# Attention and mixture of experts on one core: theta built from a row, scatters ahead of the turn's late work, unused expert rows masked on VectorE, y's zeros written later, the last layer norms through a square root

## The chip, the core and the metric

The kernel runs on one core of a Trainium2 chip. The time is device microseconds from start to end of one execution on that core; of several runs the median is given. The profile is of one further execution, taken by the hardware profiler.

## What is computed

Sixteen sequences of 512 tokens, 128 channels, all float32. The reference, cut to what matters:

```python
q = silu(x @ Wq); k = silu(x @ Wk); v = x @ Wv           # 16 heads of 8
q, k = lrpe(q), lrpe(k)                # concat(t * cos(pos * theta), t * sin(pos * theta))
out = ((q @ k.T) * tril) @ v           # no softmax
out = layernorm((out @ Wo) * sigmoid(x @ G1 @ G2)) * gamma + beta
x1 = layernorm(x + out)
logits = (x1 * rsqrt(mean(x1 * x1) + eps)) @ router_w.T   # 8 experts
topk_p, topk_i = top_k(softmax(logits), 2); rw = topk_p / sum(topk_p)
# each expert takes, in token order, its first capacity = 1280 tokens
routed[token] += rw * (silu(xg @ rg) * (xg @ ru)) @ rd    # xg: the expert's rows
shared = (silu(x1 @ sg) * (x1 @ su)) @ sd
result = layernorm(x1 + shared + routed)
```

## The kernel before

**Stages.** The work is cut in chunks of 128 tokens, four to a sequence, NT = 64 in all. A prologue (L199 to L344) makes constants. The main loop (L737 to L778) runs the attention with t from -2 to 64 as a software pipeline: turn t projects chunk t+2 (L359: two matmuls into pq, six ScalarE operations, and on VectorE hat, the queries and keys times cosine and sine), turns over chunk t+1 (L393: transposes pt, five ScalarE copies), makes the energies of chunk t (L435: sixteen matmuls pe, four VectorE maskings et by `causal`), the values of chunk t-1 (L457: pout) and the state of chunk t+1 (L412: pst, masked on VectorE, added to the last state on POOL at L433). When a sequence's four chunks are through, a generator `after(b)` (L495) is stepped on once or twice a turn: output projection, gate, two layer norms, the mean square, the transposes px1 into x1T, the router's logits. The reciprocal roots there (r, r2, rms) are powers on POOL (L109, L542). `route` (L566) is a generator too, stepped by `sprinkle`, one small VectorE operation after another: softmax, the two best experts, a running count per expert, and the slot of each token's row in its two experts.

**Rows to the experts.** `scatter` (L669) sends one chunk's rows, 132 words each (128 channels, the token's number, the tag of its first expert, two weights), to their slots in `xg_dram` by an indirect DMA that POOL issues; 128 of these are needed. `scatter_behind` issues one, and may put a small multiplication (`beat`) ahead of it on POOL, which holds it until a given column is ready. In the loop the two scatters of a turn stand last, behind `advance` and `sprinkle`.

**The shared expert as filling.** `feed` is a list of short TensorE steps (gate pg, up pu, down pd; L113 to L157). `shared(t)` in the loop takes one where it is due, twice a turn. What is left over runs after the routed experts.

**Fills.** Every expert has 1280 slots, and fewer tokens may come. Before the scatters, `fill` (L350) writes `xg_dram` with `empty`, rows of zeros with 1.0e6 as their token's number (8 DMAs of 660 KB), and `y_dram` with `zero` (8 DMAs of 1 MB), both from SP's queue, one in each of the turns 0 to 15. An unused slot's row thus comes to the expert as zeros, and its result is dropped at L862 since its target lies beyond the rows of y.

**The experts** (L924 to L951). `load_expert` (L813) loads the weights and the 1280 rows `xg` of an expert. `turn_rows` (L826) transposes 512, 512 or 256 of them on TensorE (ept) and copies the result to xgT on VectorE. Each expert works in three parts of these sizes (L933); a part has four steps i, each with a gate matmul peg, an up matmul peu, a Silu on ScalarE and the product eh on VectorE (L945), and then one entry of `backs` (the down projection ped of an earlier part with its scatter home, L850) and one of `aside`. In the middle part of expert e, `aside` holds the three `turn_rows` of expert e+1 and its `targets_of` (L836: the token's target row and weight).

**The end** (L953 to L983). The rest of `feed` runs, `add_up` adds the routed rows, and `finish_lot` (L897) makes the last layer norm: statistics, reciprocal root by `rstd_of` (L105: an addition on VectorE and a power on POOL), nb, and `res` on ScalarE. Lots are of four chunks, the last sequence's of one.

**What sets the order.** `manual_schedule(engines=ORDERED)` (L199, L736, L924) makes TensorE, ScalarE, VectorE and POOL execute in the order of the program's text; ORDERED (L18) has no SP, whose DMA issues the scheduler places. Waits between engines and for buffers come from the tiles.

**The prologue's lines.** theta is loaded to all partitions at once (L201). W comes by ScalarE's queue (L204), and eight columns of each head in it are filled with the product of the gate's two factors (pg12, L308; copy at L335). POOL clears `rw_sb`, the four padded value tiles (L287 to L295), `goes_on`, `zero` and `empty`, and builds the masks. The angle table (L315 to L337) is made for chunk 0 and then for chunks 1 to 3 together, and the sines and cosines on ScalarE; copies at L338 fill in the columns that are the same.

Of the kernel before, what the change touches and what calls it, by code (L numbers as in the profile page):

```python
# [28 lines left out]
NOBODY = 1.0e6  # L29
# [6 lines left out]
C1 = 6.28125  # L36
C2 = 2029.0 / 2 ** 20
C3 = 2.0 * math.pi - C1 - C2
# [9 lines left out]
def tile_kernel(  # L48
# [37 lines left out]
    nc.gpsimd.memset(neghalf, -0.5)  # L86
    x1 = keep.tile([P, NT, R], F32, name="x1")
# [5 lines left out]
    idx = keep.tile([P, 2, NT], I32, name="idx")  # L93
    sg_sb = keep.tile([P, IS], F32, name="sg_sb")
# [10 lines left out]
    def rstd_of(var, n, eps):  # L105
        ve = small.tile([P, n], F32, tag="ve", name="ve")
        nc.vector.tensor_scalar(ve, var, eps, None, ALU.add)  # L107
        r = small.tile([P, n], F32, tag="rstd", name="rstd")
        nc.gpsimd.tensor_tensor(r, ve, neghalf[:, :n], ALU.pow)  # L109
        return r  # L110


    def shared_steps(b):  # L113
# [6 lines left out]
        def gate_half(i):  # L120
# [7 lines left out]
            h["s", i] = sl  # L128

# [30 lines left out]
    done = set()  # L160
    latest = [None]
# [15 lines left out]
    with ExitStack() as ph:  # L177
# [21 lines left out]
        with tc.manual_schedule(engines=ORDERED):  # L199
            th_sb = cst.tile([P, D + HALF], F32, name="th_sb")  # L200
            nc.sync.dma_start(th_sb, theta.partition_broadcast(P))  # L201
# [3 lines left out]
            load_xT(0)  # L205
            g1t_sb = cst.tile([8, D], F32, name="g1t_sb")
            nc.scalar.dma_start(g1t_sb, g1t)
            g2_sb = cst.tile([8, D], F32, name="g2_sb")
            nc.scalar.dma_start(g2_sb, g2)
# [7 lines left out]
            nc.gpsimd.memset(rw_sb, 0.0)  # L217
# [3 lines left out]
            load_x(1)  # L221
# [3 lines left out]
            nc.sync.dma_start(bet, beta.partition_broadcast(P))  # L225

# [19 lines left out]
            expi = cst.tile([P, E], I32, name="expi")  # L246
            nc.gpsimd.iota(expi, pattern=[[1, E]], base=0, channel_multiplier=0)
            expf = cst.tile([P, E], F32, name="expf")
            nc.vector.tensor_copy(expf, expi)
            first = cst.tile([P, E], F32, name="first")  # L250
            nc.vector.tensor_scalar(first, expf, -1.0, float(E), ALU.mult, ALU.add)
            startrow = cst.tile([P, E], F32, name="startrow")
            nc.vector.tensor_scalar(startrow, expf, float(CAP), float(-NSLOT), ALU.mult, ALU.add)
            count = cst.tile([P, E], F32, name="count")
            nc.vector.memset(count, 0.0)
            goes_on = {}
            for n in sorted({(b1 - b0) * NC for b0, b1 in groups}):
                goes_on[n] = cst.tile([P, E, n + 1], F32, name=f"goes_on{n}")
                nc.gpsimd.memset(goes_on[n], 1.0)
                nc.gpsimd.memset(goes_on[n][:, :, 0], 0.0)  # L260


            ones = cst.tile([P, P], F32, name="ones")
            nc.vector.memset(ones, 1.0)

            causal = cst.tile([P, 3, HALF], F32, name="causal")
            nc.gpsimd.memset(causal, 1.0)
            for block, at in ((0, 0), (0, HALF), (1, HALF), (2, 0)):
                rows = causal[at : at + HALF, block, :]
                nc.gpsimd.affine_select(  # L270
                    rows, rows, pattern=[[1, HALF]], compare_op=ALU.is_ge, fill=0.0, base=0, channel_multiplier=-1
                )
            tri = cst.tile([P, P], F32, name="tri")
            nc.gpsimd.affine_select(
                tri, ones, pattern=[[1, P]], compare_op=ALU.is_gt, fill=0.0, base=0, channel_multiplier=-1
            )
# [7 lines left out]
            )  # L284


            NVP = 4  # L287
            vpads = []
            for i in range(NVP):
                vp = cst.tile([P, 4, 4, 40], F32, name=f"vpad{i}")  # L290
                nc.gpsimd.memset(vp, 0.0)

                vl = cst.tile([P, 8, 40], F32, name=f"vlow{i}")
                nc.gpsimd.memset(vl, 0.0)
                vpads.append((vp, vl))  # L295


            toki = cst.tile([P, NT], I32, name="toki")
            nc.gpsimd.iota(toki, pattern=[[P, NT]], base=0, channel_multiplier=1)
            zero = hp.tile([P, 4 * N], F32, tag="h", name="zero")  # L300
            nc.gpsimd.memset(zero, 0.0)
            empty = hp.tile([P, NS, R], F32, tag="h", name="empty")
            nc.gpsimd.memset(empty, 0.0)
            nc.gpsimd.memset(empty[:, :, D], NOBODY)


            pg = ps_w.tile([P, D], F32, tag="w", name="pg12")
            nc.tensor.matmul(pg, g1t_sb, g2_sb, start=True, stop=True)  # L308

            cst_tok = cst.tile([P, NC, 2, 16, 2, 8], F32, name="cst_tok")
            scratch = hp.tile([P, 2, NC, D + HALF], F32, tag="h", name="scratch")
            ang, turns_ = scratch[:, 0], scratch[:, 1]
            for c0, c1 in ((0, 1), (1, NC)):  # L315
# [6 lines left out]
                for part in (C1, C2, C3):  # L322
                    nc.vector.scalar_tensor_tensor(a, k, -part, a, ALU.mult, ALU.add)
# [26 lines left out]
        def fill(i):  # L350
            if i < 8:
                nc.sync.dma_start(y_rows[:, i, :], zero)
            elif i < 16:
                nc.sync.dma_start(x_rows[:, i - 8, :], empty.rearrange("p r d -> p (r d)"))
# [674 lines left out]
```

## Time and profile before

| what | us |
|---|---|
| median of 3 runs (888.18 to 888.76) | 888.75 |
| the profiled execution | 912.27 |
| its span | 910.6 |
| busy in the span: TensorE matmul (PE) | 843.0 (93%) |
| TensorE weight load (PEld, beside matmuls) | 576.5 (63%) |
| VectorE (DVE) | 557.1 (61%) |
| ScalarE (ACT) | 442.3 (49%) |
| GpSimd (POOL) | 344.2 (38%) |

The mean granted TensorE clock of that execution was 0.981. DMA moved 62.97 MB. In the trace the first energies (pe) start at 25.4, the experts' first peg at 534.3, and the last addition of routed rows on VectorE (to x1T) ends at 888.8.

The page's rows of digits cut the span into 40 equal slices; a digit is the busy share in tenths. A line of a stretch gives from and to, its length, the busy time and count of instructions of PE, PEld, DVE, ACT and POOL, the granted clock, the DMA engines' busy share and GB/s. A line of the timeline gives start, duration, engine, line and operation, out<-in, shapes, and in brackets how long the engine had been idle and what it waited for. TensorE's weight loads (LDWEIGHTS) stand apart from their matmuls; PE and SP are TensorE and SyncE.

### The profile page before, as it was taken

The page shows a single profiled execution, that of the slowest core. Times are in us where ns is not written, and L with a number is a line of the kernel's source. Part 1 is how long each engine was busy: PE and PEld are TensorE (multiplying, and loading weights), DVE is VectorE, ACT ScalarE, POOL GpSimd, SP SyncE. Part 2 cuts the span into 40 slices and gives each one's busy share as a digit, 9 for nine tenths or more (in the row PEclk, how much of TensorE's full clock was granted, in tenths as well). Part 3 has the DMA queues.
Part 4 walks back from the last instruction along what each step waited for, and adds up shares of the span by engine and source line. Part 5 has one row for each costly group of instructions (what it writes and reads, how often), then busy time and mean ns, then how long its engine had stood idle before and what let it go on. Part 6 is the DMA issues. An engine that isn't in the chain of part 4 may idle for free.

```text
span 910.6 us, 24496 instructions
## 1 busy us (share of the span) xinstructions
PE 843.0 (93%) x9790; PEld 576.5 (63%) x9790; DVE 557.1 (61%) x1687; ACT 442.3 (49%) x1285; POOL 344.2 (38%) x455
## 2 busy tenths in 40 slices
PE   2898999999998999989999999999999999999990
PEld 1676667666755776674566657776677766666670
DVE  6588788987688788878743333333333325884542
ACT  3677677566576757745522223333333332334332
POOL 4023222155655645566666703333333331010011
PEclk9999999999999999999999999999999999999996
DMA  8941111011111111000000053222231004641001
GB/s 288 417 146 33 31 32 32 24 34 55 44 50 50 55 32 39 26 22 22 12 8 2 2 159 94 77 68 60 84 91 62 27 24 125 177 135 34 25 24 46
DMA packets 64338, 62.97 MB, mean 69 GB/s; under 512 B 6179, under 2 KB 55130, under 8 KB 63200
## 3 DMA queue, kind: packets, MB, share of 16 engines
q1 hardware_dynamic: 57392, 50.44, 17.5%
q0 software_dynamic: 6656, 10.69, 3.7%
q8 instruction: 77, 1.26, 0.6%
q14 instruction: 37, 0.30, 0.1%
q10 hardware_dynamic: 176, 0.27, 0.1%
HBM read 32.71 MB, written 31.88 MB: 71 GB/s over the span
## 4 chain that ended last, share of the span: by engine, by line
PE 78%; DVE 14%; issue 3%; ACT 3%; DMA 1%; POOL 0%; POOLq 0%; DVEq 0%; ACTq 0%
PE pd L143 11%; PE pg L125 11%; PE pu L133 11%; PE ped L856 8%; PE peg L940 8%; PE peu L942 8%; PE pe L444 4%; PE pq L363 4%; DVE et L451 4%; PE pout L486 3%; PE pt L399 2%; PE pout L477 2%; PE pout L468 1%; PE po L501 1%; DVE st L101 1%
## 5 line engine op out<-in xcount | busy, mean ns | idle before, releaser
L109 POOL TENSOR_TENSOR rstd<-ve,neghalf 128x4 f32<-128x4 f32 (+1 forms) x51 | 52.4, 1028 | 259.0 <-DVE ve L107 224.0
L671 POOL DMA_INDIRECT xg_dram<-x,idx x128 | 132.2, 1033 | 37.7 <-issue 32.1
L127 ACT ACTIVATE sl<-pg 128x512 f32<-128x512 f32 x128 | 76.0, 596 | 127.6 <-PE pg L125 113.2
L862 POOL DMA_INDIRECT y_dram<-y,to x80 | 77.6, 970 | 154.2 <-ACT y L860 154.2
L945 DVE TENSOR_TENSOR eh<-esl,peu 128x512 f32<-128x512 f32 (+1 forms) x96 | 57.5, 599 | 128.1 <-PE peu L942 123.7
L125 PE MATMUL pg<-x1T,sg_sb 128*128 128x512 f32 x256 | 134.0, 605 | 2.1 <-DVE h L134 0.9
L451 DVE TENSOR_TENSOR et<-pe,causal 128x384 f32<-128x384 f32 x256 | 124.4, 547 | 18.0 <-PE pe L444 17.8
L134 DVE TENSOR_TENSOR h<-sl,pu 128x512 f32<-128x512 f32 x128 | 87.6, 684 | 75.5 <-PE pu L133 57.6
L133 PE MATMUL pu<-x1T,su_sb 128*128 128x512 f32 x256 | 131.4, 595 | 0.4 <-DVE x1T L148 0.4
L143 PEld LDWEIGHTS pd<-sd_sb,h 128*128 128x128 f32 x1024 | 119.6, 193 | 5.5 <-issue 5.5
L143 PE MATMUL pd<-sd_sb,h 128*128 128x128 f32 x1024 | 122.6, 276 | 0.0
L856 PEld LDWEIGHTS ped<-rd,eh 128*128 128x128 f32 x640 | 84.0, 192 | 24.6 <-issue 22.7
L940 PE MATMUL peg<-xgT,rg 128*128 128x512 f32 (+1 forms) x192 | 84.6, 522 | 0.0
L942 PE MATMUL peu<-xgT,ru 128*128 128x512 f32 (+1 forms) x192 | 84.4, 521 | 0.0
L856 PE MATMUL ped<-rd,eh 128*128 128x128 f32 x640 | 84.3, 275 | 0.0
L944 ACT ACTIVATE esl<-peg 128x512 f32<-128x512 f32 (+1 forms) x96 | 50.5, 526 | 56.0 <-PE peg L940 53.9
L133 PEld LDWEIGHTS pu<-x1T,su_sb 128*128 128x128 f32 x256 | 46.1, 192 | 45.8 <-issue 39.3
L860 ACT ACTIVATE y<-ped,wt 128x128 f32<-128x128 f32 x80 | 29.4, 367 | 84.6 <-PE ped L856 79.9
L125 PEld LDWEIGHTS pg<-x1T,sg_sb 128*128 128x128 f32 x256 | 44.8, 193 | 39.0 <-issue 33.9
L363 PE MATMUL pq<-W,xT 128*128 128x384 f32 x128 | 61.5, 564 | 7.8 <-DVE W L335 6.9
L444 PE MATMUL pe<-q,kT 32*64 32x192 f32 x2048 | 61.9, 338 | 0.8 <-issue 0.8
L386 DVE TENSOR_TENSOR hat<-qk,cst_tok 128x512 f32<-128x512 f32 x64 | 45.5, 711 | 23.3 <-ACT qk L371 22.6
(164 smaller groups left out, 1285.6 us busy)
## 6 DMA issues: line engine op xcount, KB each, us to landing
y_dram<-zero SPq DMA_DIRECT2D x8, 1024.0 KB
y<-y_dram SPq DMA_DIRECT2D x32, 256.0 KB, 3.2
xT<-xt SPq DMA_DIRECT2D x16, 384.0 KB, 6.5
xg_dram<-empty SPq DMA_DIRECT2D x8, 660.0 KB, 15.7
xg<-xg_dram SPq DMA_DIRECT2D x8, 660.0 KB
x<-x SPq DMA_DIRECT2D x16, 256.0 KB, 4.6
o<-res SPq DMA_DIRECT2D x15, 256.0 KB, 2.3
xg_dram<-x,idx POOLq DMA_INDIRECT x128
```

The costliest lines, as they stand in the source:

```text
L125: nc.tensor.matmul(pg, sg_sb[:, ts(i, P)], seq, start=True, stop=True)
L133: nc.tensor.matmul(pu, su_sb[:, ts(i, P)], seq, start=True, stop=True)
L134: nc.vector.tensor_tensor(h[i // half][:, i % half, :], h.pop(("s", i)), pu, ALU.mult)
L143: nc.tensor.matmul(pd, h[k][:, i - k * half, ts(c, P)], sd_sb[:, i, :], start=(i == 0), stop=(i == IS // P - 1))
L363: nc.tensor.matmul(pq[:, :, 0:24], xts[b][:, c, 0:P], W[:, 0:384].rearrange("p (h n) -> p h n", n=24), start=True, stop=True)
L444: nc.tensor.matmul(pes[g][mine, s], kT[rows, s, mine], q2[rows, s, 3 * i : 3 * i + 3], start=(s == 0), stop=(s == 1),)
L451: nc.vector.tensor_tensor(et.rearrange("p s k n -> p s (k n)"), pes[g].rearrange("p s k n -> p s (k n)"), causal.rearrange("p k n -> p (k ...
L671: i = nc.gpsimd.indirect_dma_start(out=xg_dram[:, :], out_offset=bass.IndirectOffsetOnAxis(ap=idx[:, k, t : t + 1], axis=0), in_=x1[:, t, ...
L856: nc.tensor.matmul(pd, h[:, i, ts(c, P)], got[e][2][:, i, :], start=(i == 0), stop=(i == IR // P - 1))
L862: i = nc.gpsimd.indirect_dma_start(out=y_dram[:, :], out_offset=bass.IndirectOffsetOnAxis(ap=to[:, at : at + 1], axis=0), in_=y, in_offset ...
L940: nc.tensor.matmul(pg[:, :n], rg_sb[:, ts(i, P)], xgTs[e][:, ds(o0, n)], start=True, stop=True)
L942: nc.tensor.matmul(pu[:, :n], ru_sb[:, ts(i, P)], xgTs[e][:, ds(o0, n)], start=True, stop=True)
```

## The change

**Prologue.** theta comes as one row (`th_row`) and is spread by a matmul with a row of ones into PSUM (pth) and copied to th_sb by ScalarE. The gate's factors are loaded by SP, and the first xT in two pieces, chunk 0 ahead. POOL clears two of the four value pads, ScalarE the other two (`nought`), and the copy into W goes from VectorE to ScalarE. The angles are made per chunk with nine operations in place of the old ones: chunks 0 and 1 in the prologue, 2 and 3 at the head of turns 0 and 1; sines of chunk 1 in turn -1. The masks that the energies need come first on POOL; the routing's constants (`constants_of_routing`: expf, first, startrow, count, goes_on, tri, toki, slotno) move to the end of turn 2.

**Fills and masks.** `xg_dram` is filled no longer; `y_dram` still is, by 16 DMAs of 512 KB from a tile of zeros of 256 columns that is read four times. The calls stand in the loop behind the attention (the `while`). In `turn_rows` a mask `ok` per expert compares the slot's number with the expert's `count`; an AND on VectorE clears the unused rows of xg in place ahead of their transposes, and an OR in `targets_of` sets the unused slots' targets to at least 1 << 20.

**Scatters.** In a turn they move ahead of `advance` and `sprinkle`.

**Last roots.** Once the last gate step of the shared expert has been issued (`warm_root` then asks ScalarE for a square root), `finish_lot` takes a square root on ScalarE and a reciprocal on VectorE in place of the addition and the power, and yields once less.

```diff
-NOBODY = 1.0e6
+NOBODY = 1 << 20
...
+    count = keep.tile([P, E], F32, name="count")
+    slotno = keep.tile([P, NS], F32, name="slotno")
+    zero = keep.tile([P, N // 2], F32, name="zero")
...
+    def rstd_by_root(var, n):
+
+        root = small.tile([P, n], F32, tag="ve", name="root")
+        nc.scalar.activation(root, var, AF.Sqrt, bias=eps_col)
+        r = small.tile([P, n], F32, tag="rstd", name="rstd")
+        nc.vector.reciprocal(r, root)
         return r
...
+            if (b, i) == (B - 1, IS // P - 1):
+
+                warm_root = small.tile([P, 1], F32, tag="warm_root", name="warm_root")
+                nc.scalar.activation(warm_root, eps_col, AF.Sqrt)
+                roots.append(warm_root)
...
-            th_sb = cst.tile([P, D + HALF], F32, name="th_sb")
-            nc.sync.dma_start(th_sb, theta.partition_broadcast(P))
+            th_row = cst.tile([1, D + HALF], F32, name="th_row")
+            nc.sync.dma_start(th_row, theta.unsqueeze(0))
 
             W = cst.tile([P, 512], F32, name="W")
             nc.scalar.dma_start(W, wqkv)
-            load_xT(0)
             g1t_sb = cst.tile([8, D], F32, name="g1t_sb")
-            nc.scalar.dma_start(g1t_sb, g1t)
+            nc.sync.dma_start(g1t_sb, g1t)
             g2_sb = cst.tile([8, D], F32, name="g2_sb")
-            nc.scalar.dma_start(g2_sb, g2)
+            nc.sync.dma_start(g2_sb, g2)
+            xts[0] = wk2.tile([P, NC, P + HALF], F32, tag="xT", name="xT_0")
+            nc.sync.dma_start(xts[0][:, 0:1], xt[0, :, 0:1])
+            nc.sync.dma_start(xts[0][:, 1:], xt[0, :, 1:])
...
-            nc.gpsimd.memset(rw_sb, 0.0)
+            nc.vector.memset(rw_sb, 0.0)
...
+                if i < 2:
+                    nc.gpsimd.memset(vp, 0.0)
+                    nc.gpsimd.memset(vl, 0.0)
...
+            def nought(tile_, n):
+                nc.scalar.copy(tile_, zcol.to_broadcast([P, n]))
+
+            pth = ps_w.tile([P, D + HALF], F32, tag="w", name="pth")
+            nc.tensor.matmul(pth, ones[0:1, :], th_row, start=True, stop=True)
+            th_sb = cst.tile([P, D + HALF], F32, name="th_sb")
+            nc.scalar.copy(th_sb, pth)
...
+            for vp, vl in vpads[2:]:
+                nought(vp.rearrange("p a b d -> p (a b d)"), 640)
+                nought(vl.rearrange("p a d -> p (a d)"), 320)
+            nc.scalar.copy(
+                W[:, 0:384].rearrange("p (h n) -> p h n", n=24)[:, :, 8:16], pg.rearrange("p (h d) -> p h d", d=8)
+            )
...
+            turns_of = cst.tile([P, D + HALF], F32, name="turns_of")
+            nc.vector.tensor_scalar(turns_of, pth, 1.0 / (2.0 * math.pi), None, ALU.mult)
+
+        def angles(c, th):
+
+            a, size, k, whole = scratch[:, c], scratch[:, NC + c], scratch[:, 8], scratch[:, 9]
+            both = ((slice(0, D), pos[:, 0, c : c + 1]), (slice(D, D + HALF), pos[:, 1, c : c + 1]))
+            for m, at in both:
+                nc.vector.tensor_scalar(k[:, m], turns_of[:, m], at, MAGIC, ALU.mult, ALU.add)
+            nc.vector.tensor_scalar(whole, k, MAGIC, -C1, ALU.subtract, ALU.mult)
+            for m, at in both:
+                nc.vector.scalar_tensor_tensor(a[:, m], th[:, m], at, whole[:, m], ALU.mult, ALU.add)
+            nc.vector.tensor_scalar(k, k, MAGIC, -C2, ALU.subtract, ALU.mult)
+            nc.vector.tensor_tensor(a, a, k, ALU.add)
+            nc.vector.scalar_tensor_tensor(size, a, -1.0, a, ALU.mult, ALU.max)
+            nc.vector.tensor_scalar(a, a, -PI_BELOW, PI_BELOW, ALU.max, ALU.min)
+
+        def sines(c):
+
+            for s, (from_, scale, bias) in enumerate([(scratch[:, NC + c], -1.0, half_pi), (scratch[:, c], 1.0, 0.0)]):
+                for to, n0, n1 in ((cst_tok[:, c, 0], 0, D), (cst_tok[:, c, 1, 1::2], D, D + HALF)):
+                    nc.scalar.activation(
+                        to[:, :, s, :], from_[:, n0:n1].rearrange("p (h d) -> p h d", d=8), AF.Sin,
+                        scale=scale, bias=bias,
+                    )
+
+        def same(c):
+
+            nc.vector.tensor_copy(
+                cst_tok[:, c, 1, 0::2].rearrange("p h s d -> p h (s d)"),
+                cst_tok[:, c, 0, 0::2].rearrange("p h s d -> p h (s d)"),
+            )
+
+        with tc.manual_schedule(engines=ORDERED):
+            angles(0, pth)
+            sines(0)
+            angles(1, th_sb)
+            same(0)
...
+        def constants_of_routing():
...
-            zero = hp.tile([P, 4 * N], F32, tag="h", name="zero")
-            nc.gpsimd.memset(zero, 0.0)
-            empty = hp.tile([P, NS, R], F32, tag="h", name="empty")
-            nc.gpsimd.memset(empty, 0.0)
-            nc.gpsimd.memset(empty[:, :, D], NOBODY)
...
-            for c0, c1 in ((0, 1), (1, NC)):
-                a, k = ang[:, c0:c1, :], turns_[:, c0:c1, :]
-                for c in range(c0, c1):
-                    nc.vector.tensor_scalar(ang[:, c, 0:D], th_sb[:, 0:D], pos[:, 0, c : c + 1], None, ALU.mult)
-                    nc.vector.tensor_scalar(ang[:, c, D:], th_sb[:, D:], pos[:, 1, c : c + 1], None, ALU.mult)
-                nc.vector.tensor_scalar(k, a, 1.0 / (2.0 * math.pi), MAGIC, ALU.mult, ALU.add)
-                nc.vector.tensor_scalar(k, k, MAGIC, None, ALU.subtract)
-                for part in (C1, C2, C3):
-                    nc.vector.scalar_tensor_tensor(a, k, -part, a, ALU.mult, ALU.add)
-                nc.vector.tensor_scalar(a, a, -PI_BELOW, PI_BELOW, ALU.max, ALU.min)
-                nc.vector.scalar_tensor_tensor(k, a, -1.0, a, ALU.mult, ALU.max)
...
+        def beginning(t):
+
+            if t == -1:
+                sines(1)
+            elif t == 0:
+                angles(2, th_sb)
+                sines(2)
+            elif t == 1:
+                angles(3, th_sb)
+                sines(3)
+
+        def beginning_done(t):
+            if t == 1:
+
+                nought(zero, N // 2)
+            elif t == 2:
+                constants_of_routing()
...
-        y_rows = y_dram.rearrange("(p q r) d -> p q (r d)", p=P, r=4 * N // D)
-        x_rows = xg_dram.rearrange("(p q r) d -> p q (r d)", p=P, r=NS)
...
+            nc.gpsimd.iota(sloti, pattern=[[P, NS]], base=0, channel_multiplier=1)
+            nc.vector.tensor_copy(slotno, sloti)
...
+        y_rows = y_dram.rearrange("(p q r s) d -> q p r (s d)", p=P, r=4, s=N // 2 // D)
 
         def fill(i):
-            if i < 8:
-                nc.sync.dma_start(y_rows[:, i, :], zero)
-            elif i < 16:
-                nc.sync.dma_start(x_rows[:, i - 8, :], empty.rearrange("p r d -> p (r d)"))
-
+            nc.sync.dma_start(y_rows[i], zero.unsqueeze(1).to_broadcast([P, 4, N // 2]))
+
+        fills = list(range(2 * T * D // (P * 2 * N)))
...
+            if 0 < t < NC:
+                same(t)
...
+                beginning(t)
...
-                if 0 <= t < 16:
-                    fill(t)
...
+                if left:
+
+                    scatter_behind(oTs[(t - 1) // NC][:, ds((t - 1) % NC * P, 1)])
+                    scatter_behind()
                 advance(turns, "narrow")
                 advance(turns)
                 sprinkle(t, 4)
-                if left:
-
-                    scatter_behind(oTs[(t - 1) // NC][:, ds((t - 1) % NC * P, 1)])
-                    scatter_behind()
+                beginning_done(t)
...
-            while turns or todo or scatters or over:
-                if not (turns or todo or scatters):
...
+                if t % 4 == 1 and fills:
+                    fill(fills.pop(0))
...
+            if o0 == 0:
+
+                ok = ep.tile([P, 2, NS], I32, tag="ok", name=f"ok_{e}")
+                nc.vector.tensor_scalar(ok[:, 0], slotno, count[:, e : e + 1], -1.0, ALU.is_lt, ALU.mult)
+                nc.vector.tensor_scalar(ok[:, 1], slotno, count[:, e : e + 1], float(NOBODY), ALU.is_ge, ALU.mult)
+                taken[e] = ok
+            here = slice(o0 // P, (o0 + n) // P)
+            rows = xg[:, here, :].bitcast(I32)
+            nc.vector.tensor_tensor(
+                rows, rows, taken[e][:, 0, here].unsqueeze(2).to_broadcast([P, n // P, R]), ALU.bitwise_and
+            )
...
+            nc.vector.tensor_tensor(to, to, taken[e][:, 1], ALU.bitwise_or)
...
-            rs = rstd_of(mv[:, :, 1], n, LN_EPS)
+
+            rs = rstd_by_root(mv[:, :, 1], n) if roots else rstd_of(mv[:, :, 1], n, LN_EPS)
             yield True
-            yield True
+            if not roots:
+                yield True
...
```

## The prediction

> **What bounds the kernel now.** I read the page's 40 slices first, then busy time by stretch, then the timeline of the two stretches where the change puts work on a chain.
>
> ```profile
> PE   2898999999998999989999999999999999999990
> DVE  6588788987688788878743333333333325884542
> 0.00:25.00 25.00, 8.57 (x37) 5.72 (x38) 17.12 (x42) 9.44 (x37) 10.82 (x40) 1.00 0.88 301
> 25.00:60.00 35.00, 31.41 (x797) 23.22 (x796) 24.24 (x59) 24.22 (x94) 4.47 (x6) 0.95 0.80 319
> 100.00:200.00 100.00, 97.44 (x2011) 67.70 (x2010) 88.63 (x282) 71.25 (x244) 26.82 (x30) 1.00 0.11 33
> 200.00:300.00 100.00, 92.29 (x1775) 63.80 (x1774) 78.28 (x251) 64.65 (x218) 56.50 (x69) 0.98 0.16 48
> 540.00:650.00 110.00, 110.00 (x556) 77.17 (x555) 39.10 (x81) 40.44 (x89) 38.79 (x40) 1.00 0.27 78
> 889.00:911.00 22.00, 0.00 (x0) 0.00 (x0) 6.50 (x37) 5.16 (x12) 4.20 (x6) 0.60 0.14 38
> ```
>
> Columns of the stretches: from:to, length, busy PE, PEld, DVE, ACT, POOL, then the clock, DMA share, GB/s. TensorE (PE) is the bound from about 25 us to 889: the reader should see 110.00 busy of 110 in the experts' stage, where VectorE is busy 39 and so has much spare time. Only two stretches are not TensorE's: the first 25 us, where it works 8.6, and the last 22. So time is won at the two ends, and any wait put into TensorE's stream between them costs its full length.
>
> The second look is at one turn of the experts, at the place where the next expert's rows are transposed:
>
> ```profile
> 545.22 1.02 PE L942 MATMUL peu<-xgT,ru 128*128 128x512 f32 x2
> ...
> 546.08 1.05 PE L856 MATMUL ped<-rd,eh 128*128 128x128 f32 x8
> ...
> 546.35 0.69 DVE L945 TENSOR_TENSOR eh<-esl,peu 128x512 f32<-128x512 f32 x1 [1.10 <-PE peu L942]
> 546.86 0.47 PEld L833 LDWEIGHTS ept<-ident,xg 128*128 128x128 f32 x4
> ```
>
> Here the transposes (ept) start straight behind the four matmuls of ped, at 546.86, while VectorE is still in eh until 547.04. They wait for nobody.
>
> **What the Trainium skill says.** "VectorE: DVE Perf Modes", The perf-mode tier table: a two-tensor operation on fp32 runs at one element a cycle, the double mode being for single-source operations. The trace agrees: 128x512 out of SBUF alone took 683 ns (L889), and eh 688. The AND is a two-tensor operation on 32-bit words, so I price its 528 elements at 0.71 us and the 264 at 0.42 (L945's 128x256: 421 ns). "TensorE: Matmul & The Clock Gate", Part 1: an idle window of some 3.4 us halves TensorE's clock. The trace agrees only loosely: a stop of 1.8 us at 38.4 was already followed by a mean clock of 0.66 in 40 to 45, a stop of 0.9 at 531.8 by none. "ScalarE: Activation LUTs", What ACT_TABLE_LOAD costs: a set switch takes a load of about 1.28 us (1283 ns in the trace).
>
> **The change part by part.** The built order of instructions is part of the evidence. TensorE's sequence is the same but for one small matmul; the number of shared-expert steps ahead of the experts is unchanged, so every stage keeps its cover.
>
> 1. *The ANDs, experts 1 to 7.* On VectorE the order is now eh, AND, copy of the transpose, where it was eh, copy. The AND writes xg, which the transposes read; queued behind the waiting transposes is all of TensorE's remaining stream. Middle third of a part: eh starts 546.35, the next operation on VectorE can start 0.60 later (L945 to the next in the trace), AND 0.71, signal to TensorE 0.10 (W copy to matmul at the start): 547.76, against 546.86, so 0.90 us. First third: eh at 543.31, + 0.60, two small ok operations (0.10, then 0.17 and a wait of 0.02), AND 0.71, 0.10: 545.01 against 543.82, so 1.19. Last third: 549.40 + 0.60 + 0.42 + 0.10 = 550.52 against 549.91, so 0.61. Together 2.70 per expert, seven times: **+18.9**. Bounds: +14 if the AND runs in a double mode after all (0.42 instead of 0.71), +21 with 0.1 more at each of the 21 signals. Below zero is excluded: nothing is removed from that chain. The OR on the targets (0.17) lies beside matmuls: nothing; without cover 0.17 each.
>
> 2. *The ANDs of expert 0.* No eh lies between; transposes and copies alternate through two PSUM buffers. Before, weights for peg load at 534.34. Now the chain from the last h (532.61) is: first AND lands earlier, since xg_0 (issued 525.90, 350 GB/s from 528) is in by about 530; but AND stands in front of three h, which then run 0.7 later; then transpose 0.6, copy 0.75, AND 0.7, transpose 0.7, copy 0.7, AND 0.4, transpose 0.4: about 537.7, so 3.3 later, and some 5 us of little work may halve the clock for a while (up to 1.7). I take **+4** (2.5 to 5.5).
>
> 3. *The start.* Before, theta (96 KB spread over 128 partitions) lands at 6.06, VectorE's first operations take 2.84 and 1.9 us beside POOL's memsets (later 0.28), W is ready at 14.2, the first hat ends at 20.8, and the first energies start at 25.4. Now theta is one row and one matmul, POOL has two pads before its memsets stop, and only chunk 0's nine operations (about 0.3 each) stand ahead. Estimate: theta's row 3.1, matmul 3.9, ScalarE's copy 4.3, angles ready at 7.1; ScalarE clears two pads (1.8) and copies W at 6.3 (W itself landed at 6.3 before, and now has less beside it); first projection 2.1, its six ScalarE operations 1.1, sines 1.0, hat 11.5, ScalarE's turn_over until 14.6, first energies at 16.1: 9.3 earlier. Of this the next two turns give back: angles(2), angles(3), each some 2.8 on VectorE and 1.0 of sines on ScalarE, and the routing constants (about 0.7): energies(2) come at 27.7, 4.5 earlier than 32.2. The fills then count: before, 13.6 MB at 410 GB/s held the DMA engines from 12 to 53 us, and TensorE has four stops of 0.2 to 1.8 us and a slow clock there. SP is not in the ordered set, so its 16 zero fills (8.4 MB) do not stand behind the attention but behind the fifth load of x and the third of xT, from about 28 us; xT for sequence 3 queues behind eleven of them, with 20 us to spare. I expect half of the stops to go (2 to 3). **-6** (-10 to -2).
>
> 4. *Attention.* The two scatters of a turn (1.03 each) now stand ahead of the pow of r2 and rms on POOL, which thus come up to 2.4 later; their readers follow a turn (5 us) later. The state's add on POOL, which the values wait for, gets the scatters out of its way earlier. **-1** (-5 to +3).
>
> 5. *The end.* Two lots of four and four single chunks remain after TensorE's last result, in the order of before too:
>
> ```profile
> 890.54 0.18 DVE L103 BATCH_NORM_AGGREGATE mv<-st 128x2 f32<-128x6 f32 x1
> 890.76 0.17 DVE L107 TENSOR_SCALAR ve<-mv 128x4 f32<-128x4 f32 x1
> 891.10 1.01 POOL L109 TENSOR_TENSOR rstd<-ve,neghalf 128x4 f32<-128x4 f32 x1 [6.09 <-DVE ve L107]
> 892.14 0.16 DVE L910 SCALAR_TENSOR_TENSOR nb<-mv,rstd 128x4 f32<-128x4 f32 x1 [1.21 <-POOL rstd L109]
> ```
>
> From statistics (890.72) to nb it is 1.42; by root (0.21, like the smallest ScalarE copies), reciprocal (0.18) and signals about 0.53: 0.89 less, twice. A root queues behind the previous lot's res on ScalarE: for the lots that fits (1.5 against 1.6 of statistics); the first single chunk waits for four res and loses 0.7; three others gain 0.47. The table load (1.28) lies beside the last down matmuls. -1.8 + 0.7 - 1.4 = **-2.5** (-4 to -1).
>
> Sum: 18.9 + 4 - 6 - 1 - 2.5 = +13.4. The profiled execution took 912.27 us (span 910.6), 2.6% more than the median; the sum on it gives 925.7. These are waits, not a rate, so I put the same 13.4 on the median of 888.75: **902.2**.
>
> **Rivals.** *DMA traffic, faster.* TensorE's stops that wait for nothing shown (pout 6.6 and 4.8, pst 3.4, pe 0.8, pq 0.4: 16 us) lie where DMA is full or scatters run. If traffic holds up TensorE's instructions and the change ends all of it (with 1 us of slow clock), it is worth 17 in place of my 3.5 in parts 3 and 4, and the rest of the start 7.5: 888.75 + 22.9 - 2.5 - 7.5 - 17 = 884.7. It decides once these stops give back over 13. Against: all 128 scatters remain and the fills still fall into the attention.
> *Slow clock, slower.* If the 1 us stops plus transposes halve the clock in each expert for some 3.4 us, each costs 1.7 more, 12 in all: 914. Against: the clock is 1.00 after the 0.9 stop at 531.8.
> *The ANDs do not stop TensorE* because something reorders them: no; the built order on both engines shows eh, AND, transposes.
>
> **Chances.** Forecast 0.81 (its own range 895 to 909); traffic 0.08; slow clock 0.11. Of the forecast a few hundredths reach below: faster by over 0.2% (about what a measurement of this kernel can tell from no change) 0.08, within 0.2% 0.04, slower 0.88. For 8 in 10 I take 892 to 911: most of the forecast, with the start's and attention's good bounds below and the lower part of the slow clock above.
>
> **What would show it.** Transposes (ept) waiting for the AND some 0.6 to 1.2 us each, TensorE about 93% busy in the experts' stage instead of 100; first energies near 16 us; last reciprocal to end shorter by 2 to 3. Wrong: ANDs of 0.4 us or less, a clock under 1 in the experts, or TensorE busy over 97% in 200 to 450.

## The result, and the profile after

The changed kernel takes 894.28 us (median of 6 runs, 892.57 to 898.58) against 888.43 for the kernel before (6 runs beside it): a ratio of 1.0073, 95% interval 1.0051 to 1.0096. It is slower, as forecast, but by 5.9 us and not by 13.4.

In three sets of runs the kernel before takes 887 to 891 us and in three others 906 to 913 (below: the first and the second sort), so that times are compared within one sort only. The comparison above is of the first sort, and the profiled execution shown with the prediction (912.27) fits the second; below, a new profile of the kernel before from a set of the first sort (span 886.1, the first experiment) stands in its place. The expectations put the difference down to the chip, but the last two sets, one of each sort, were on chips of the same number, so what makes the sort is not known.

The changed kernel's busy tenths in 40 slices, and its stretches (columns as in the prediction):

```profile
PE   5889999999989998999999799999999999999993
DVE  7788888988898988887333344334433423886544
0.00:25.00 25.00, 15.22 (x196) 9.73 (x197) 18.91 (x67) 17.22 (x64) 6.06 (x26) 0.97 0.56 172
25.00:60.00 35.00, 30.81 (x861) 23.64 (x860) 28.61 (x84) 25.51 (x100) 8.94 (x19) 0.98 0.79 273
100.00:200.00 100.00, 97.79 (x2012) 68.13 (x2010) 87.52 (x275) 72.88 (x250) 33.58 (x40) 1.00 0.12 35
200.00:300.00 100.00, 93.71 (x1969) 68.74 (x1972) 87.84 (x284) 71.31 (x238) 60.83 (x74) 1.00 0.17 52
512.00:622.00 110.00, 102.19 (x514) 71.19 (x513) 44.41 (x101) 36.37 (x81) 34.91 (x36) 1.00 0.23 68
878.70:892.30 13.60, 0.00 (x0) 0.00 (x0) 6.43 (x36) 6.56 (x18) 0.00 (x0) 0.67 0.19 58
```

The reader should see three things: TensorE has 15.2 us of work in the first 25, where it had 8.6; in the experts' stage it is busy 102.2 of 110, where it was busy all the time; and the last stretch, from the last addition of rows to the end, is 13.6 long with GpSimd (POOL) at 0.00. The same stretch of the kernel before, in its new profile:

```profile
864.70:886.20 21.50, 0.00 (x0) 0.00 (x0) 6.35 (x36) 5.17 (x12) 4.20 (x6) 0.56 0.13 37
```

It is 21.5 long. Marks read from the timelines of these two profiles, in us from the span's start, give the whole account (a hat is counted by its chunk; where the expectations say turn 32, the hat of chunk 32 is meant):

| mark | before | changed | difference | step since the mark above |
|---|---|---|---|---|
| first hat starts (chunk 0) | 20.13 | 10.09 | -10.0 | -10.0 |
| hat of chunk 16 | 91.58 | 81.70 | -9.9 | +0.1 |
| hat of chunk 32 | 185.75 | 175.90 | -9.85 | 0.0 |
| last hat | 375.52 | 366.83 | -8.7 | +1.2 |
| last h ahead of the experts ends | 508.17 | 500.40 | -7.8 | +0.9 |
| first peg | 510.00 | 504.73 | -5.3 | +2.5 |
| last ped ends | 729.34 | 743.35 | +14.0 | +19.3 |
| last addition of rows ends | 864.67 | 878.68 | +14.0 | 0.0 |
| last res ends | 877.68 | 889.70 | +12.0 | -2.0 |
| span ends | 886.11 | 892.23 | +6.1 | -5.9 |

How an AND stands in TensorE's way, in the changed kernel's timeline, middle third of expert 0's middle part:

```profile
519.32 0.69 DVE L1021 TENSOR_TENSOR eh<-esl,peu 128x512 f32<-128x512 f32 x1 [1.10 <-PE peu L1018]
519.93 0.70 DVE L901 TENSOR_TENSOR xg<-xg,ok 128x528 int32<-128x528 int32 x1
520.74 0.42 PEld L906 LDWEIGHTS ept<-ident,xg 128*128 128x128 f32 x4 [0.83 <-PE ped L930]
520.77 0.63 PE L906 MATMUL ept<-ident,xg 128*128 128x128 f32 x4 [0.67 <-DVE xg L901]
```

The AND starts 0.61 after eh and takes 0.70, as the forecast had it (0.60 and 0.71), and the transposes come 0.11 behind its end. Matmuls stand still for 0.67; the whole step is longer by 0.86, where 0.90 was forecast: 3.90 from one group of transposes to the next, against 3.04 in the kernel before. The period from one expert to the next is 29.73, where it was 27.20.

And the end, first the changed kernel, then the one before:

```profile
888.46 0.28 ACT L119 ACTIVATE root<-mv,eps_col 128x1 f32<-128x1 f32 x1
888.77 0.16 DVE L121 RECIPROCAL rstd<-root 128x1 f32<-128x1 f32 x1 [0.37 <-ACT root L119]
888.97 0.16 DVE L986 SCALAR_TENSOR_TENSOR nb<-mv,rstd 128x1 f32<-128x1 f32 x1
889.21 0.49 ACT L989 ACTIVATE res<-x1T,nb,rstd 128x128 f32<-128x128 f32 x1 [0.47 <-ACT root L119]
```

```profile
876.37 0.54 POOL L109 TENSOR_TENSOR rstd<-ve,neghalf 128x1 f32<-128x1 f32 x1 [0.97 <-DVE ve L107]
876.94 0.16 DVE L910 SCALAR_TENSOR_TENSOR nb<-mv,rstd 128x1 f32<-128x1 f32 x1 [0.75 <-POOL rstd L109]
877.19 0.49 ACT L913 ACTIVATE res<-x1T,nb,rstd 128x128 f32<-128x128 f32 x1 [1.02 <-DVE nb L910]
```

Both timelines end there, yet the span goes on for 2.5 us in the first (to 892.2) and for 8.4 in the second (to 886.1). The views leave out what they don't count as work; the trace's own records show it. At the end of each engine's instructions stands one called DRAIN, and GpSimd's is long:

```
kernel                 GpSimd's last power ends   DRAIN starts   takes   ends     last res ends   span ends
before (new profile)   876.91                     876.34         8.99    885.33   877.68          886.11
changed                865.23                     864.20         9.46    873.65   889.70          892.23
```

Its record starts together with GpSimd's last instruction, here a power, and ends 8.42 us after that instruction has ended, in both. In the kernel before it is over 7.7 us after the last res, and the span ends 0.78 later. In the changed kernel GpSimd has nothing to do after the last of the early lots, and its DRAIN lies under other work.

### The profile page after: what moved, and what is told of

Its sections match the earlier page's. It is cut to its first block, busy times and chain, and to the rows that moved or that the text cites. A ratio compares the mean times of both kernels' runs of the same rounds, so it can differ in the third digit from the quotient of the medians.

```text
span 892.2 us, 24564 instructions
## 1 busy us (share of the span) xinstructions
PE 829.3 (93%) x9792; PEld 566.0 (63%) x9792; DVE 570.5 (64%) x1754; ACT 446.8 (50%) x1301; POOL 334.2 (37%) x443
## 5 line engine op out<-in xcount | busy, mean ns | idle before, releaser
L137 PE MATMUL pg<-x1T,sg_sb 128*128 128x512 f32 x256 | 132.0, 597 | 1.7 <-ACT sl L139 0.7
L113 POOL TENSOR_TENSOR rstd<-ve,neghalf 128x4 f32<-128x4 f32 x44 | 47.1, 1071 | 195.6 <-DVE ve L111 169.3
L419 PE MATMUL pq<-W,xT 128*128 128x384 f32 x128 | 59.3, 546 | 4.7 <-ACT vlow L440 2.6
```

Of the source, the lines that this page charges most:

```text
L137: nc.tensor.matmul(pg, sg_sb[:, ts(i, P)], seq, start=True, stop=True)
```

## The experiments

**The kernel before, profiled again** (no edit).

> The kernel before, unchanged, profiled a second time. My theory: the first profile of it (span 910.6) holds some 22 us that its ordinary executions do not have, with 8.5 of them between the last res and the end, the rest in the attention's second half (the hats drift from 12.4 to 29.2 us behind the changed kernel's between turns 32 and 63); an ordinary profile then ends near 886 to 888 of span, with 0.0 to 0.3 us more per turn in turns 32 to 63 than the changed kernel, not 0.55. Rival: the second half is truly that slow in every execution, and the scatters' new place is worth 17 us; then the drift shows again.

887.82 us (one execution; 11 others beside it: 888.91), span 886.1. The second half of the attention is not slow in this execution: from the hat of chunk 32 to the last hat it takes 189.8 us (185.75 to 375.52), as in the changed kernel (190.9), where the first profile had 207.8. The 8.4 us behind the last res are there again, though, so that part of the expectation was wrong: they belong to the kernel.

**ANDs a step ahead of their transposes.** `turn_rows` is split; its ok and AND become `clear`.

```diff
-    aside = [lambda q=q: turn_rows(e + 1, *q) for q in parts] + [lambda: targets_of(e + 1)]
+    aside = [lambda: clear(e + 1, *parts[0]),
+             lambda: (turn_rows(e + 1, *parts[0]), clear(e + 1, *parts[1])),
+             lambda: (turn_rows(e + 1, *parts[1]), clear(e + 1, *parts[2])),
+             lambda: (turn_rows(e + 1, *parts[2]), targets_of(e + 1))]
```

> The changed kernel, with each AND of experts 1 to 7 placed on VectorE one step of the middle part ahead of its transposes, and the transposes one step later than they were. My theory, that the ANDs stand in TensorE's path behind eh: the period from one expert to the next goes from 29.73 back to 27.2, seven times 2.53 is 17.7 us, so about 876.5 and faster than the kernel before by 1.3%. Rival, that VectorE or the arrival of the rows is then late anyway (the first AND is now asked for 3.4 us after the middle part begins at the earliest): less than 9 us come back.

876.11, ratio to the kernel before 0.9852 (0.9838 to 0.9866). First TensorE's waits from 505 us to the end of the experts in the changed kernel, then in this one (what it waited for, total, times, longest):

```profile
PE ept L906 <- DVE xg L901: 7.4, 14, 0.7
PE ept L906 <- ACT y L934: 5.4, 6, 0.9
PE ept L906 <- PE ped L930: 0.9, 1, 0.9
```

```profile
PE ept L910 <- DVE xg L899: 2.6, 2, 1.4
```

The 21 waits are gone (the two left are expert 0's). A wait put down to y or ped is one for the AND all the same, since it goes too when only the ANDs are moved. From first peg to last ped it is 221.0, against 238.6. The ANDs' price was in their place, not in VectorE's time.

**Expert 0's ANDs ahead as well**, on top of that:

```diff
             for o0, n in parts:
                 clear(0, o0, n)
+            for o0, n in parts:
                 turn_rows(0, o0, n)
```

> The version with the ANDs a step ahead, and expert 0's three ANDs all ahead of its transposes as well. Theory: expert 0's 4.3 us between the last h and its first gate matmul fall to the 1.8 of the kernel before, and the slow clock behind it (first two gate and up pairs 1.6 longer) goes too: 4 less than 876.1, 872. Rival: the three h behind the ANDs are 1.2 later and TensorE waits for them instead: 875.

This ran in a set of the second sort: 881.91 against 909.05 for the kernel before, 0.9683 (0.9663 to 0.9702), so only the marks are set beside the version above. From the last h to the first peg it is 1.8 (4.2 there), from the first peg to the last ped 219.3 (221.0), like the kernel before. But one up matmul of the shared expert (pu) waits 2.0 for an h that stands behind the ANDs, where it waited 1.0 in the changed kernel. So some 3 of the 4 are saved.

```profile
PE pu L150 <- DVE h L151: 2.0, 1, 2.0
```

Of these 3, the 1.7 behind the first peg is a slow clock that did not come in this profile. It is not sure to stay away: in the next version, with the same ANDs, the clock is halved from 509.26 to 512.67, and the stretch takes 220.1.

**The tile of zeros late**, on top of both: `nought(zero, N // 2)` at t == NT - 4 in place of t == 1, which puts the 16 fills of y behind all loads of x in SP's queue.

> The version with all ANDs a step ahead (of expert 0 too), with the tile of zeros made in turn 60 in place of turn 1, so that the 16 fills of y stand behind all loads of x in SP's queue and run near 360 us, not near 30. Theory: TensorE's stops between 30 and 50 us (some 2.5 us in the changed kernel's profile) go, and the later traffic costs nothing: 19 + 2.5, so 21 to 22 us below the changed kernel beside it (the ANDs alone: 21.8). With the ANDs of experts 1 to 7 worth 17.7 and expert 0's worth 4.1 this makes 24.3 below. Rival, that the fills then hold up the scatters or TensorE at 360 us as much: 21.8 below.

880.46 against 910.52, 0.9670 (0.9653 to 0.9688); the changed kernel beside it took 902.02, so 21.6 less. That is the rival's number, and not told apart from the version above (0.9683): the fills' place is worth nothing that shows.

**Powers for the last roots**, in the changed kernel: the lines with `warm_root` are left out, so `roots` stays empty.

> The changed kernel, with the last layer norms' reciprocal roots by addition and power as before. My theory: the end is longer by 2.3 (13.3 from the last addition to x1T to the end of the last res in the profile before, 11.0 in the one after), so 896.6. Rival, that the end is set by the statistics and the outputs alone: no difference, 894.3.

903.68, ratio 1.0164 (1.0146 to 1.0182): 9.4 more than the changed kernel's 894.28 in another set of the first sort, not 2.3. By the profiles, whose spans differ by 10.3, it is 13.0 from the end of the last addition to the last res (11.0 in the changed kernel; the 13.3 of the expectation counts from 888.8, given above as that addition's end in the first profile, but there it starts at 888.83 and ends at 889.12), and from there to the end 8.4 (2.5). These two make 7.9. The rest, 2.4, stands ahead of the last addition already (881.04 against 878.68), 2.3 of it at the hat of chunk 32 (178.16 against 175.90), up to where the two kernels do not differ.

**The roots alone, on the kernel before** (`rstd_by_root`, `warm_root` and `finish_lot` as in the change).

> The kernel before with the change of the last roots alone. The records of the trace show GpSimd's closing DRAIN: in the kernel before it starts 1.3 us before the last res ends and takes 8.99 us, so that the span ends 8.4 after the last res; in the changed kernel GpSimd's last work is some 25 us earlier, its DRAIN (9.46) is over before the outputs, and the span ends 2.5 after the last res. My new theory: the roots save this (5.9) and the 2.0 ahead of the last res, 7.9 in all, so 881.0. My forecast's own term, 2.5 for the end: 886.4. Rival, that something else in the changed kernel (its output DMAs, a lighter DMA load) made the end short: 886 to 887.

In a set of the second sort: 903.58 against 909.05, 0.9927 (0.9911 to 0.9942), that is 6.6 less (5.3 to 8.1). By the marks the last res ends 11.0 after the last addition and the span 2.6 later, 13.6 in place of 21.5: the 7.9 of the theory, with nothing else of the change present.

**One late instruction on GpSimd**, in the changed kernel:

```diff
+            if lot[1] == NT:
+                late = small.tile([P, 1], F32, tag="late", name="late")
+                nc.gpsimd.tensor_tensor(late, nb, neghalf[:, 0:1], ALU.mult)
```

> The changed kernel with one added multiplication of 128x1 on GpSimd, which waits for the nb of the last chunk and which nobody reads. If GpSimd's closing DRAIN takes some 9 us behind its last instruction whatever this was: the last res at 889.7 as before, the DRAIN from about 889.3 to 898.3, the span's end near 898.5, so 900.5 (6.2 slower than 894.3). If the 9 us belong to the power and not to any late instruction: no difference, 894.3.

In the same set as the last: 908.33 (kernel before 909.05). The end of its timeline:

```profile
897.13 0.19 POOL L989 TENSOR_TENSOR late<-nb,neghalf 128x1 f32<-128x1 f32 x1 [23.99 <-DVE nb L986]
897.14 0.49 ACT L992 ACTIVATE res<-x1T,nb,rstd 128x128 f32<-128x128 f32 x1 [0.48 <-ACT root L119]
```

The span ends at 906.5, 8.9 after the last res; the records have GpSimd's DRAIN from 897.10 on, 8.65 long, so that it ends 8.42 after the multiplication. By the end of the profile (8.9 in place of 2.5) an unread multiplication of 0.19 us costs 6.4: the power has no part in it, the place of GpSimd's last instruction has.

**The prologue of the kernel before**, in the changed kernel (without `empty`, and with the small tile of zeros).

> The changed kernel with the prologue of the kernel before (theta to all partitions by one DMA, the pads and constants on GpSimd ahead of the loop, angles of chunks 1 to 3 together); masks, fills of y, scatters and roots as changed. By the marks of the two ordinary profiles the changed kernel's first hat is 10.0 earlier, the fourth turn's 5.5, the last hat 8.7, the last h 7.8. Theory, that the prologue is worth all of this: 902 (7.8 slower). Rival, that the fills that are gone from turns 8 to 15 and the smaller ones give a good part of it: 2 to 4 slower, since the stops between turns 4 and 8 of the kernel before would be gone here too.

908.25, in the set in which the changed kernel with the late instruction took 908.33. Without the 6.4 of that instruction this would be some 902, so by this estimate it is 6.2 slower. The hats, against that kernel: the first +7.6, chunk 4 +2.6, chunks 8, 16 and 32 +6.3, +5.9, +5.9. So the prologue makes some 6 of the 10.

**The fills of xg_dram back**, in the changed kernel (8 DMAs of 660 KB in turns 8 to 15, from zeros that one ScalarE operation writes in turn 1; ANDs kept).

> The changed kernel with the 8 fills of xg_dram (660 KB each, from a tile of zeros that ScalarE makes in turn 1) back in the text's turns 8 to 15, and the ANDs kept. Theory: of the 7.8 that the changed kernel's attention is ahead by, some 5.5 are the prologue's (run with the prologue of before) and some 2 the fills', as stops of TensorE between 25 and 60 us: 2 slower than the changed kernel beside it. Rival, that the DMA traffic of the fills is hidden in both: no difference (under 1). Second rival, that 13.8 MB in the first 70 us delay the loads of x too: over 5 slower.

905.87, against 902.02 for the changed kernel beside it: 3.9 slower, and by the hats 1.9 at chunk 4, where the added ScalarE operation has its part, and 4.0 at chunk 8. This lies between the theory and its second rival. With the prologue's 6.2 it makes the 10 of chunk 16, but what the added operation costs is not the fills', so that the two explain 8 to 10.

**Scatters in the old place**, in the changed kernel (the `if left:` block with the two calls back behind `sprinkle(t, 4)`), three times, and **in the new place alone, on the kernel before**, twice.

> The changed kernel, with the two scatters of a turn back behind advance and sprinkle. My forecast: 1 us slower (between 3 faster and 5 slower), 895.3. Rival, that the scatters' place makes what the two first profiles differ by in turns 32 to 63: 10 to 17 us slower, 904 to 911. Third: the change of place costs instead of gaining, since the powers of r2 and rms come later; then 1 to 3 us faster.

894.87, ratio 1.0074 (1.0056 to 1.0093): no difference to the changed kernel's 1.0073. That set was of the first sort.

**The changed kernel again**, beside the two fills runs:

> The changed kernel itself, beside the two others of this set on one chip. Where the kernel before takes some 889, it should be near 894 again (0.6 to 0.7% slower). Where the kernel before takes some 909, the added GpSimd operation of the earlier run (908.3) less its 6.3 gives 902, 0.8% faster: on that chip the kernel before has stops of TensorE in turns 32 to 63 that the changed one has not.

902.02 against 910.52, ratio 0.9908 (0.9887 to 0.9929). In a set of the second sort the change makes the kernel faster. The scatters' place once more:

> The kernel before with the scatters alone moved ahead of advance and sprinkle. On a chip where the kernel before takes some 889, no difference (within 1 of 889), as the changed kernel with the scatters moved back showed none. On a chip where it takes some 909: my theory, that the scatters' place makes the stops of pout and pst there (turns 32 to 63 last 208 us in the kernel before and with only its roots changed, 194 in all kernels with the scatters ahead), gives 13 to 14 less, 896. Rival, that another part or the mere shift of the stream in time does it: under 3 less.

> The changed kernel with the scatters back in their old place, a second time, since the first was on a chip where the kernel before takes some 889 and showed nothing (turns 32 to 63: 189.7 against 190.9). If this chip is one where it takes some 909: my theory gives 13 to 14 more than the 902 of the changed kernel, 915; the rival that the place does not matter there either, 902. If it is one of 889: 895 again.

A set of the first sort: 888.15 against 888.48 (0.9998, 0.9986 to 1.0010), and 896.08 (1.0090, 1.0071 to 1.0108). No difference, as theory and rival both had it for such a set. Then, in one of the second:

> As the last time but one (the kernel before with the scatters alone moved ahead), which was on a chip where the kernel before takes 888.5 and showed no difference, as expected there. On a chip of the other sort: my theory 896, the rival 906 to 910. On one of the same sort nothing new, and the point stays open.

> As the last one (the changed kernel with the scatters in their old place). On a chip where the kernel before takes some 909: my theory 915, the rival 902. On one of 889: 895.

895.01 against 909.94 (0.9842, 0.9820 to 0.9863), and 914.28 (1.0050, 1.0034 to 1.0067), near the theory's 896 and 915. TensorE's waits for nothing that the profile shows ("issue"), in the second half of the attention, largest first; in the first profile of the kernel before (186 to 400 us) and then with the scatters ahead (186 to 380):

```profile
PE pout L486 <- issue: 5.6, 13, 0.5
PE pst L422 <- issue: 3.4, 9, 0.4
PE pout L477 <- issue: 2.2, 6, 0.4
```

```profile
PE pout L477 <- issue: 0.8, 4, 0.3
```

Where these stops lie, in the first profile of the kernel before:

```profile
254.65 1.08 PE L486 MATMUL pout<-et,vpad 128*32 128x64 f32 x32
254.84 1.04 POOL L671 DMA_INDIRECT xg_dram<-x,idx  x1 [0.17 <-issue]
...
256.14 0.35 PE L422 MATMUL pst<-vpad,hat 128*32 128x64 f32 x6 [0.41 <-issue]
...
256.18 0.97 POOL L671 DMA_INDIRECT xg_dram<-x,idx  x1 [0.30 <-issue]
...
256.93 0.32 PE L422 MATMUL pst<-vpad,hat 128*32 128x64 f32 x4 [0.44 <-issue]
...
257.66 0.35 PE L422 MATMUL pst<-vpad,hat 128*32 128x64 f32 x6 [0.41 <-issue]
```

Small matmuls come in bursts of some six, 0.75 apart, about the two scatters. In the records from the hat of chunk 32 to the last hat, 29 matmuls of pout and pst start over 0.3 us after the one before, and 27 of these gaps touch a scatter; with the scatters ahead 5 such gaps are left. pout or pst run during a scatter for 13.5 us in the old order and 2.7 in the new one. But in the new profile of the kernel before, of the first sort, it is 15.0 us in the old order and there is no such gap. So to lie side by side is not enough, and what else it takes stays open.

## Why the prediction missed, step by step

1. *ANDs, experts 1 to 7: right.* Forecast +18.9; the period is 2.53 longer, seven times, 17.7, and moving the ANDs alone gave it back.
2. *Expert 0: right, a little short.* Forecast +4 (2.5 to 5.5). The first AND waits for the rows, and two h stand behind it:

```profile
497.12 0.71 DVE L901 TENSOR_TENSOR xg<-xg,ok 128x528 int32<-128x528 int32 x1 [3.58 <-DMA xg<-xg_dram]
498.48 1.12 PE L150 MATMUL pu<-x1T,su_sb 128*128 128x512 f32 x2 [0.97 <-DVE h L151]
```

   From the last gate matmuls of the shared expert to these it is 2.00, where it was 0.86: 1.1 later (0.7 was forecast). First peg is then 2.5 later behind the last h, and 1.6 of the 19.3 that follow goes to a slow clock: in the kernel with the old prologue, whose trace has no slow clock there, first peg to last ped takes 237.1 in place of 238.6, which is the kernel before's 219.3 and 17.7. Together this is 5.2. The 3.4 us after the first peg have a granted clock of about half (from and to, length, then PE to POOL, clock, DMA):

```profile
500.40:504.70 4.30, 1.59 (x10) 1.17 (x11) 2.34 (x4) 0.00 (x0) 0.00 (x0) 0.98 0.02 5
504.70:508.10 3.40, 3.40 (x7) 1.43 (x6) 1.19 (x7) 0.60 (x1) 0.00 (x0) 0.52 0.20 32
508.10:511.50 3.40, 3.40 (x10) 1.49 (x9) 1.38 (x2) 1.19 (x2) 0.00 (x0) 1.00 0.57 167
```

   The clock's record has the half from 504.54 to 507.95, 3.41 us. This agrees with the Trainium skill, "TensorE: Matmul & The Clock Gate", Part 1, in the length of the window, some 3.4 us. The page has the half clock follow an idle window; the stretch ahead of it here was not idle, with 1.59 us of matmuls in 4.30. The rival of a slow clock at every expert's AND fell: the clock is 1.00 in 512 to 622.
3. *The start: right in kind, too small.* Forecast -6 (-10 to -2); -9.9 at the hat of chunk 16. The first energies start 11.4 earlier (24.85 to 13.46), not 9.3. What the next chunks give back (5.5 is left at chunk 4) returns by chunk 8, about half of it by the fills (4.0 less 1.9 us with them back).
4. *Attention: within its bounds.* Forecast -1 (-5 to +3); from chunk 16 to the last h it is +2.1, of which 1.1 is expert 0's (step 2), so +1.0, on the other side of nothing. What makes it is not known; the scatters' place has no part that shows in sets of the first sort. In those of the second sort it is worth -12 to -15: there the rival of stops without a releaser decides, at the 13 us from which it was said to, and the change makes the kernel faster. So the sign of the forecast came true in the sort that was measured; in the sort that its profile came from it would not have, and this term was too small there by more than ten. That it did not count is luck. The rival's cause was half right: not DMA traffic in general (the fills, put back, cost 3.9), but the place of the scatters in the turn.
5. *The end: this step failed.* Forecast -2.5, measured -7.9. Up to the last res it was -2.0, near what was worked out. The term that the sum lacked, and so put at nothing, is what lies behind the last res: the span of the first profile ends 8.4 after it (902.13 to 910.56). The outputs need 2.5 of that, as the changed kernel shows, and the remaining 5.9 were GpSimd's DRAIN, which ends under other work once the last power is off that engine. The forecast counted the powers' latency (0.5 to 0.9 each) and not when GpSimd is done. The roots alone on the kernel before, the powers back in the changed one, and the unread multiplication all show it. The Trainium skill, "VectorE: DVE Perf Modes", The DRAIN you can't avoid, speaks of DRAINs of some 12 ns from the preamble and postamble, on all five engines; GpSimd's at the end of this program is not of that size, with 8,650 to 9,460 ns, and the measurement decides.

The sum on the marks: 17.7 + 5.2 - 8.9 (steps 3 and 4) - 7.9 = +6.1, the difference of the two spans. Of the 7.3 us between this and the forecast's 13.4, 5.4 are step 5 and 1.9 steps 3 and 4; steps 1 and 2 make up for each other, 1.2 below and 1.2 above.

The profile that the sum was made on and the times that it was put on were 2.6% apart. The forecast took the terms over as if they were the same on both. For one of them, the scatters, that does not hold.

## What to carry to other kernels

Read the profile to the end of the span, not to the last instruction with a name: if the span goes on for more than an output takes, ask which engine closes last, and let GpSimd finish well before the others. Here it is free if its last instruction ends some 6.7 us before the last res does (an estimate from the profiles: 8.42 of DRAIN and 0.78 to the span's end, less the 2.5 of the outputs). An operation that has to be inserted on a path between two engines costs its full time where its input comes last; one step earlier in the same queue it cost nothing that shows. With the ANDs of experts 1 to 7 so placed the changed kernel is 1.5% faster than the kernel before, where it was 0.7% slower (and, with expert 0's ahead too, 3.2% to 3.3% faster in sets of the second sort). A profile whose time is off from the runs by some per cent may show stops that those runs don't have; take a second one before a term rests on it.

## What the runs showed of the hardware

GpSimd's closing DRAIN ends 8.42 us after GpSimd's last instruction in all 17 profiles, be that a power of four columns (1.01 us), a power of one (0.54) or a multiplication of one (0.19). Its record starts with that instruction and so is 8.65 to 9.46 long. All these kernels issue indirect DMAs from GpSimd; whether it is as long without them was not tried. And the same kernel takes 888 to 889 us in some sets of runs and 909 to 911 in others, with most of the difference (18.0 of 24.5 us between the two profiles) between the hat of chunk 32 and the last, where small matmuls and indirect DMAs of GpSimd lie side by side; with the scatters elsewhere in the turn it takes 888 in one sort and 895 in the other. Why the sorts differ is not known.
